# Two equal parts of 16 tiles, q rows of the first part made inside attention, and the last norm on ScalarE

## The chip, the core and the metric

The kernel runs on one core of a Trainium2 chip. The metric is the device time of one execution in microseconds (us), and the median over 13 executions is 1920.35 us. The core has five engines that each work through their own queue in order: TensorE (PE, with its weight loads as PEld), VectorE (DVE), ScalarE (ACT), GpSimd (POOL) and SyncE (SP, which only starts transfers). DMA engines move data between the chip's memory (DRAM) and the on-chip SBUF; TensorE writes to PSUM.

## The reference

One layer of a graph network over 4096 nodes of 512 features, 8 heads of 64. All arithmetic is in float32.

```python
hs = layer_norm(x) * ln1_scale + ln1_bias          # 4096 x 512
ht = layer_norm(h_target) * ln1_scale + ln1_bias
q = (ht @ Wq + bq) / 8;  k = hs @ Wk + bk;  v = hs @ Wv + bv
logits = where(adj != 0, q . k per head, -1e30)     # adj: 4096 x 4096, some 17 edges a row
ctx = softmax(logits) @ v
ht = layer_norm(ht + ctx @ Wo + bo) * ln2_scale + ln2_bias
y = ht + gelu(ht @ W1) @ W2                         # W1 512 x 2048, W2 2048 x 512
out = layer_norm(x + y)                             # no scale, no bias
```

A row of adj has few edges, so the kernel does not form the logits. It makes a list of the neighbours of each target row and gathers their k and v rows.

## The kernel before, in words

**Tiles and parts.** A tile is 128 target rows. The 32 tiles' rows are in two parts: part A, the first 20 tiles of rows, and part B, the last 12. Within a part the rows are sorted by their number of edges, so that the rows of one tile need about the same number of gathers. CAPS_A and CAPS_B are the numbers of gathers for each tile of a part (600 in all). Tiles are taken in groups of two (the first and the last group have one): A tiles with few edges first, then those with more, then B.

**First phase.** Three streams are woven into one program by hand-given costs (`_weave`; each `yield` gives a cost in units, and the stream that is furthest behind goes next; the scheduler of the language then fixes each engine's order with this as its priority).
- `project` handles a list of pairs of tiles. For a pair of x tiles (`source`), the rows are normalised (ACT, line 800), transposed (PE, line 834), scaled and shifted (ACT, line 838), multiplied by Wk and Wv (PE, line 848), copied (ACT, line 850) and written to the table kvd in DRAM. For a pair of h_target tiles (`target`), the same transposes are multiplied by Wq (PE, line 860); DVE applies the scale and bias (line 863), two more operations make the residual rows from the normalised h (lines 868 and 869, on POOL for the first tiles and on DVE for the rest), and both halves go as one row of 1024 values to a table tqd in DRAM (line 871). The order is x pairs, then x and part A's h pairs in turn, then part B's h pairs.
- `edges` reads adj in four quarters for each tile. A quarter (128 x 1024 int32, 512 KB) goes into a tile "a" with two buffers; ACT takes its sign and the row count (line 670); DVE multiplies by an index ramp (line 672) and extracts the positions (line 674 and lines 681 to 698). The first 20 tiles are done in this phase, and more in what `fill` takes.
- `sort` ranks the rows of a part by counting (two pairs of matmuls with scans between, lines 767 to 775) and scatters their lists to DRAM by POOL (line 783).
- `moments` loads a tile of h_target ("hst") and takes its mean and variance on DVE; before, for part B's tiles alone.

When all k and v rows are in kvd and part A's lists are written, the gathers can begin.

**Second phase.** Three streams again: attention, the feed-forward (`feed`), and the lists of part B that are left (`other_lists`).
- `issue` starts the gathers of three edges' rows at a time (POOL, line 896, one gather for each edge position, 512 KB) into the tile kv with six buffers of three slots, four groups ahead of use (AHEAD). For a tile's first group it also gathers the tile's q and residual rows from tqd (`front`).
- For each group of three: DVE multiplies k by q (line 1058) and sums by head (line 1062), ACT takes exp (lines 1066 and 1076; line 1040 and the eight multiplications at line 1043 handle the third slot's v), DVE multiplies v by the weights (line 1023), and PE sums the v rows by transposes that add up in PSUM (cps, line 1031). For tiles of part B, DVE first adds two of the three v rows (line 1027), which saves PE four transposes.
- `finish`, a step at a time, divides by the sum of the weights (lines 957 to 970), multiplies by Wo into the one PSUM bank "t" (line 975), adds the residual on DVE (line 978), normalises (lines 653 and 990), and transposes to h2T (lines 999 and 1003, through "t" again).
- `feed` multiplies h2T by W1 (`hidden`, PE, line 1156), takes Gelu on ACT (line 1159), and multiplies by W2 into po (PE, line 1165). The residual is put into po first by transposes (line 1189).
- `end` adds x (DVE, line 1122), takes mean and variance on DVE (line 653), the power on POOL (line 643), scales on DVE (line 1129), and scatters the rows to the output (POOL, line 1133).

The scalars rstd of the norms are a power of -0.5 on POOL (`power`, line 643).

## Time and profile before

| | us |
|---|---|
| median of 13 runs | 1920.35 |
| lowest, highest | 1909.82, 1925.46 |
| the profiled execution | 1925.34 |
| its span | 1923.6 |
| last matmul ends, in the span | 1904.3 |
| first gather of kv starts, in the span | 405.4 |
| TensorE's first feed-forward matmul, in the span | 505.5 |

The profile is of one execution. Busy time is the time in which an engine executes; an engine that waits for another is idle. A row of a group gives the line in the kernel, the engine, the operation, tile names (out<-in), the shape, the count, the busy time in us and the mean of one in ns, then the idle time ahead of it with what ended it. A matmul of 128 x 512 in float32 shows as two records (passes). The busy time of passes is less than their count times their mean, since they overlap; costs on TensorE are therefore taken as busy time divided by the count. A row of a stretch gives its bounds, its length, and for each engine the busy time and the number of instructions, then the clock granted to TensorE, the mean busy share of the DMA engines and GB/s.

### The profile page before, as it was taken

What the parts mean: (1) busy time and instruction counts of PE and PEld (TensorE: products, weight loads), DVE (VectorE), ACT (ScalarE), POOL (GpSimd) and SP (SyncE); (2) the same over time, 40 slices, a digit from 0 to 9 for tenths busy, and PEclk for the clock granted to TensorE, in tenths of its full rate; (3) what the DMA queues carried; (4) which work ended last, traced back from release to release, by engine and by line L of the source; (5) the groups of instructions that cost most, each with busy time, mean ns of one, the idle gap of its engine ahead of it and who ended that gap; (6) DMA issues with size and microseconds to landing.
All of it is one profiled execution on the core that took longest, in us unless ns stands there. A gap on an engine that the chain in (4) does not pass through costs nothing.

```text
span 1923.6 us, 22615 instructions
## 1 busy us (share of the span) xinstructions
PE 1712.5 (89%) x6974; PEld 1101.5 (57%) x6974; DVE 1503.0 (78%) x2712; ACT 1173.8 (61%) x2937; POOL 951.4 (49%) x847
## 2 busy tenths in 40 slices
PE   7899888787789899988998999888998998999996
PEld 3344344334557566765666666666665765666664
DVE  4778887656989899866677878888999998989601
ACT  5566565444668776656575757676776776766510
POOL 1012232233545445565465656667677776677101
PEclk9999999888989999998999999999999999999998
DMA  8888886698979686757676878788888787778200
GB/s 315 267 270 290 287 267 212 207 351 340 358 285 319 244 305 225 261 180 236 198 272 237 280 245 309 264 293 290 286 300 287 263 302 263 248 260 278 80 1 24
DMA packets 155738, 490.48 MB, mean 255 GB/s; under 512 B 24900, under 2 KB 29592, under 8 KB 155608
## 3 DMA queue, kind: packets, MB, share of 16 engines
q0 software_dynamic: 99040, 355.28, 53.3%
q1 hardware_dynamic: 50864, 114.78, 17.9%
q10 hardware_dynamic: 5704, 18.89, 2.5%
q8 instruction: 57, 0.93, 0.2%
q14 instruction: 73, 0.60, 0.1%
HBM read 441.23 MB, written 47.65 MB: 254 GB/s over the span
## 4 chain that ended last, share of the span: by engine, by line
PE 30%; DVE 25%; DMA 20%; issue 10%; POOL 7%; ACT 5%; another core or an unknown queue 0%; POOLq 0%; SPq 0%; ACTq 0%; DVEq 0%
PE pf L1156 11%; PE po L1165 9%; DMA a<-in_adj_dram 9%; DVE kv L1058 7%; DMA kv<-kvd,rec 7%; DVE lg L1062 6%; PE cps L1031 5%; DVE kv L1023 4%; POOL kv L896 4%; PE t L975 2%; ACT sg L670 1%; POOL rec L783 1%; PE pq L848 1%; DMA xin<-in_L_gnn_h_target_dram 1%; DVE cand L674 1%
## 5 line engine op out<-in xcount | busy, mean ns | idle before, releaser
L896 POOL DMA_INDIRECT kv<-kvd,rec x600 | 702.0, 1170 | 407.8 <-issue 191.7
L1156 PE MATMUL pf<-h2T,w 128*128 128x256 f32 (+1 forms) x2176 | 480.3, 373 | 9.6 <-ACT h2T L1003 5.0
L1165 PE MATMUL po<-w,gt 128*128 128x512 f32 x1024 | 473.6, 601 | 8.1 <-ACT gt L1159 6.7
L1058 DVE TENSOR_TENSOR kv<-kv,tq 128x1536 f32<-128x1536 f32 (+2 forms) x210 | 351.6, 1675 | 145.1 <-DMA kv<-kvd,rec 132.7
L1156 PEld LDWEIGHTS pf<-h2T,w 128*128 128x128 f32 x2176 | 394.9, 194 | 79.5 <-issue 30.5
L1043 ACT ACTIVATE kv<-kv,pa 128x64 f32<-128x64 f32 x1512 | 387.4, 335 | 5.5 <-ACT pa L1040 0.2
L1062 DVE TENSOR_REDUCE lg<-kv 128x24 f32<-128x1536 f32 (+2 forms) x210 | 349.6, 1668 | 1.2
L1031 PEld LDWEIGHTS cps<-ident,kv 128*128 128x128 f32 x2092 | 247.4, 145 | 109.5 <-issue 47.4
L1031 PE MATMUL cps<-ident,kv 128*128 128x128 f32 x2092 | 273.9, 280 | 34.6 <-DVE kv L1023 20.6
L1165 PEld LDWEIGHTS po<-w,gt 128*128 128x128 f32 x1024 | 188.5, 193 | 194.9 <-issue 184.3
L1023 DVE TENSOR_TENSOR kv<-kv,p 128x1024 f32<-128x1024 f32 (+1 forms) x210 | 248.7, 1187 | 14.6 <-ACT p L1066 11.1
L670 ACT ACTIVATE sg<-a 128x1024 uint8<-128x1024 int32 x128 | 135.0, 1055 | 164.2 <-DMA a<-in_adj_dram 141.5
L643 POOL TENSOR_TENSOR n_rs<-n_ve,mhalf 128x2 f32<-128x2 f32 (+2 forms) x61 | 51.6, 846 | 331.2 <-DVE n_ve L636 289.3
L1066 ACT ACTIVATE p<-lg 128x24 f32<-128x24 f32 (+2 forms) x178 | 34.0, 191 | 191.6 <-DVE lg L1062 168.5
L975 PE MATMUL t<-wo,rb 128*128 128x512 f32 x256 | 124.2, 627 | 26.7 <-DVE rb L970 23.5
L848 PE MATMUL pq<-wk,hT 128*128 128x512 f32 x256 | 125.0, 633 | 24.8 <-ACT hT L838 22.8
L1159 ACT ACT_TABLE_LOAD x111 | 142.4, 1283 | 1.9
L848 PE MATMUL pq<-wv,hT 128*128 128x512 f32 x256 | 120.6, 616 | 17.8 <-DVE wd L672 9.6
L860 PE MATMUL pq<-wq,hT 128*128 128x512 f32 x256 | 124.6, 632 | 13.2 <-ACT hT L838 12.6
L1159 ACT ACTIVATE gt<-pf 128x512 f32<-128x512 f32 x128 | 76.4, 597 | 90.5 <-PE pf L1156 76.9
L674 DVE MAX8 cand<-wd 128x8 uint16<-128x103 uint16 (+1 forms) x640 | 128.6, 252 | 1.2
L1066 ACT ACT_TABLE_LOAD x82 | 105.2, 1283 | 26.2 <-DVE lg L1062 15.5
(140 smaller groups left out, 1519.4 us busy)
## 6 DMA issues: line engine op xcount, KB each, us to landing
a<-in_adj_dram SPq DMA_DIRECT2D x128, 512.0 KB
kvd<-row ACTq DMA_DIRECT2D x32, 512.0 KB
tq<-row SPq DMA_DIRECT2D x20, 512.0 KB
kv<-kvd,rec POOLq DMA_INDIRECT x600
xin<-in_L_gnn_h_target_dram SPq DMA_DIRECT2D x16, 512.0 KB
w<-in_L_gnn_W_dram SPq DMA_DIRECT2D x8, 1024.0 KB
xin<-in_x_dram SPq DMA_DIRECT2D x15, 512.0 KB
tq<-row POOLq DMA_DIRECT2D x12, 512.0 KB
```

The lines of the kernel that those rows point to most:

```text
L670: nc.scalar.activation(sg, a, AF.Sign, accum_out=dpart[:, i, h:h + 1])
L848: nc.tensor.matmul(pkv, hT[:, kc, j * P:(j + 1) * P], w[:, kc, :], start=kc == 0, stop=kc == KC - 1)
L896: nc.gpsimd.indirect_dma_start(out=dst, out_offset=None, in_=table[:, :], in_offset=bass.IndirectOffsetOnAxis(ap=idx, axis=0))
L975: nc.tensor.matmul(pa, ct[:, c, :], wo[:, c, :], start=c == 0, stop=c == KC - 1)
L1023: nc.vector.tensor_tensor(v4, v4, p[:, j0:j0 + m, :].unsqueeze(3) .to_broadcast([P, m, H, HD]), ALU.mult)
L1031: nc.tensor.matmul(cps[:, c, :], kv[:, j, D + c * P:D + (c + 1) * P], ident, is_transpose=True, start=j0 + j == 0 and c == 0, stop=j0 + n ...
L1043: nc.scalar.mul(v, v, pa[:, hd:hd + 1])
L1058: nc.vector.tensor_tensor(kv[:, :n, :D], kv[:, :n, :D], tq[:, :D].unsqueeze(1).to_broadcast([P, n, D]), ALU.mult)
L1062: nc.vector.tensor_reduce(lg[:, :n, :], kv[:, :n, :D].rearrange("p j (h d) -> p j h d", h=H), AX.X, ALU.add)
L1156: nc.tensor.matmul(pf[:, k, :], w1[(f0 + k) // KC][:, kc, (f0 + k) % KC * P:((f0 + k) % KC + 1) * P], h2T[:, kc, :w], start=kc == 0, stop= ...
L1159: nc.scalar.activation(gt, pf, AF.Gelu_apprx_tanh)
L1165: nc.tensor.matmul(po[j], gt[:, k, j * P:(j + 1) * P], w2[(f0 + k) // KC][:, (f0 + k) % KC, :], start=False, stop=f0 + k == FC - 1, skip_g ...
```

## The change

What it does, by parts:
1. The parts are 16 and 16 tiles; the caps sum to 603.
2. Only part B's q rows are made in the first phase's `project`, after all x tiles. Its residual rows come from transposing the scaled and shifted hT back on PE, and are copied by ACT; the constant bo + bv Wo is folded into the shift b1r, and its product with Wq is taken off the q bias again.
3. For a tile of part A, `front` gathers the rows of h_target itself in the tile's order, scales them on ACT by the row statistics (now carried in the list record), transposes them, and multiplies by Wq, one step at each `advance` of attention. hT stays beside q in tq. `finish` adds it by four transposes into the bank of the Wo product; ACT copies the sum out, where DVE added. The first two tiles' fronts run ahead of the gathers (EARLY).
4. `moments` runs for all 32 tiles.
5. `end` adds x with an accumulated sum, takes the variance by Square on ACT (which writes over po) and scales by Identity on ACT.
6. kv is a ring of 17 slots, not six buffers of three; adjacency quarters are asked for two ahead; wd is written over sg; gt has two buffers, not three.
7. Costs and order in the weave change; W1 and W2 quarters 2 and 3 are asked for inside the first feed-forward, on ACT's queue.

```diff
-CAPS_A = (40, 24, 23, 22, 21, 20, 20, 19, 18, 18, 17, 17, 16, 16, 15, 15, 14, 13, 12, 11)
-CAPS_B = (38, 23, 21, 20, 19, 18, 17, 16, 16, 15, 14, 12)
+CAPS_A = (39, 24, 23, 22, 20, 19, 19, 18, 17, 17, 16, 15, 15, 14, 13, 11)
+CAPS_B = (38, 24, 23, 22, 20, 19, 18, 18, 17, 17, 16, 15, 15, 14, 13, 12)
+    RING = 17
...
             def late_constants():
...
                 nc.vector.tensor_add(bob, pb, bob)
-                return wq, s1b, bob, bq8
+                yield
+                pt = psi.tile([P, D], F32, name="pq", bufs=3)
+                for kc in range(KC):
+                    nc.tensor.transpose(pt[:, kc * P:(kc + 1) * P], bob[:, kc * P:(kc + 1) * P],
+                                        ident)
...
+                nc.vector.tensor_add(b1r, rbc, b1c)
+                yield
+                pb = psi.tile([P, D], F32, name="pq", bufs=3)
+                for kc in range(KC):
+                    nc.tensor.matmul(pb, rbc[:, kc:kc + 1].to_broadcast([P, P]), wq[:, kc, :],
+                                     start=kc == 0, stop=kc == KC - 1)
+                nc.vector.tensor_sub(bqr, bqr, pb)
...
             def edges(i):
...
-                    a = lp.tile([P, QW], I32, name="a", bufs=2)
-                    nc.sync.dma_start(a, adj[i * P:(i + 1) * P, h * QW:(h + 1) * QW])
+                    n = i * NQ + h
+                    while len(adjs) < min(n + 2, NT * NQ):
+                        adjs.append(quarter(*divmod(len(adjs), NQ)))
+                    a, adjs[n] = adjs[n], None
...
-                    elif h == 3 and moms and NA - i <= len(moms) + 1:
+                    if h % 2 and moms:
                         moments(moms.pop(0))
...
             def sort(part):
...
+                yield 6.0
...
+                yield 4.0
...
-                yield 20.0
+                yield 10.0
...
                 def target(n, j):
...
+                    pr = psi.tile([P, D], F32, name="pq", bufs=3)
+                    for kc in range(KC):
+                        nc.tensor.transpose(pr[:, kc * P:(kc + 1) * P],
+                                            hT[:, kc, j * P:(j + 1) * P], ident)
...
-                    eng, dma = (nc.vector, nc.sync) if ready else (nc.gpsimd, nc.gpsimd)
-                    eng.tensor_mul(tq[:, D:], t[:, j, :], s1b)
-                    eng.tensor_add(tq[:, D:], tq[:, D:], bob)
...
+                    nc.scalar.copy(tq[:, D:], pr)
+                    r0 = (g * G + j - NA) * P
+                    nc.sync.dma_start(tqd[r0:r0 + P, :], tq)
...
             def front(i):
...
+                rec = recs[i]
+                tq = sp.tile([P, 2 * D], F32, name="tq", bufs=3)
+                if TILES[i][0] >= NA * P:
+                    gather(tq, tqd, rec[:, ROW:ROW + 1])
+                    tqs[i] = tq
                     return
...
+                t = tq[:, :D]
+                gather(t, h_target, rec[:, TGT:TGT + 1])
+                yield
+                m = rec[:, RST:RST + 2].bitcast(F32)
+                nc.scalar.activation(t, t, AF.Identity, bias=m[:, 1:2], scale=m[:, 0:1])
+                yield
+                pt = ps.tile([P, KC, P], F32, name="t")
+                for kc in range(KC):
+                    nc.tensor.transpose(pt[:, kc, :], t[:, kc * P:(kc + 1) * P], ident)
+                hT = tq[:, D:].rearrange("p (c t) -> p c t", c=KC)
+                for kc in range(KC):
+                    nc.scalar.activation(hT[:, kc, :], pt[:, kc, :], AF.Identity,
+                                         bias=b1r[:, kc:kc + 1], scale=s1c[:, kc:kc + 1])
+                yield
+                yield
+                pq = ps.tile([P, D], F32, name="t")
+                for kc in range(KC):
+                    nc.tensor.matmul(pq, hT[:, kc, :], wq[:, kc, :], start=kc == 0,
+                                     stop=kc == KC - 1)
+                nc.vector.scalar_tensor_tensor(tq[:, :D], pq, HD ** -0.5, bqr,
+                                               op0=ALU.mult, op1=ALU.add)
                 tqs[i] = tq
...
-                kvs[k] = kp.tile([P, S, 2 * D], F32, name="kv")
+                kvs[k] = ring[:, place[k]:place[k] + n, :]
...
             def finish(i, p, cps, group, hs, mv):
...
+                first = TILES[i][0] < NA * P
+                if first:
+
+                    for c in range(KC):
+                        nc.tensor.matmul(pa[:, c * P:(c + 1) * P],
+                                         tq[:, D + c * P:D + (c + 1) * P], ident,
+                                         is_transpose=True, start=c == 0, stop=False,
+                                         skip_group_check=True)
...
-                nc.vector.tensor_add(h, pa, tq[:, D:])
+                if first:
+                    nc.scalar.copy(h, pa)
+                    yield
+                else:
+                    nc.vector.tensor_add(h, pa, tq[:, D:])
...
                 def advance():
+                    for i in list(fronts):
+                        step(fronts, i)
...
             def end(group, xs, po):
...
-                    nc.vector.tensor_add(xs[j], po[j], xs[j])
-                    stats(sp, xs[j], mv[:, j, :], "n3")
...
+                    nc.vector.scalar_tensor_tensor(xs[j], xs[j], 1.0, po[j], op0=ALU.mult,
+                                                   op1=ALU.add, accum_out=sm[:, j, 0:1])
+                nc.vector.tensor_scalar_mul(sm[:, :nt, 0], sm[:, :nt, 0], -1.0 / D)
                 yield
                 for j in range(nt):
-                    nc.vector.tensor_scalar(xs[j], xs[j], mv[:, j, 0:1], rs[:, j:j + 1],
-                                            op0=ALU.subtract, op1=ALU.mult)
+                    nc.scalar.activation(po[j], xs[j], AF.Square, bias=sm[:, j, 0:1],
+                                         accum_out=sm[:, j, 1:2])
...
+                for j in range(nt):
+                    nc.scalar.activation(xs[j], xs[j], AF.Identity, bias=nm[:, j:j + 1],
+                                         scale=rs[:, j:j + 1])
...
                 last = hidden(0)
+                if g == 0:
+                    load_quarter(wp2, 2, nc.scalar)
...
+                    if len(w1) < 4:
+                        load_quarter(wp2, 3, nc.scalar)
...
+            EARLY = 2
+            PAUSE = 30.0
+            ROWS = 8.0
...
-                    yield 1.9 * cost
+                    yield 1.5 * cost
                 yield from sort(1)
...
-            _weave((att, t0), (chain(feed(g) for g in range(len(GROUPS))), UNIT / 2 + LEAD),
-                   (other_lists(), t0))
+            _weave((att, t0 + PAUSE), (chain(feed(g) for g in range(len(GROUPS))), UNIT / 2 + LEAD),
+                   (other_lists(), t0 - 30.0))
```

## The prediction

> **What bounds the kernel now.** I read the page first, for the busy shares; then the same engines in seven stretches; then one source line in those stretches, for a rate; then what TensorE waited for.
>
> ```profile
> span 1923.6 us, 22615 instructions
> PE 1712.5 (89%) x6974; PEld 1101.5 (57%) x6974; DVE 1503.0 (78%) x2712; ACT 1173.8 (61%) x2937; POOL 951.4 (49%) x847
> ```
>
> TensorE is busy 1712.5 of 1923.6 us, so the span is its work plus 211 us of idling. The stretches say where it idles (columns: stretch, length, busy time of PE, PEld, DVE, ACT, POOL, granted clock, DMA share, GB/s):
>
> ```profile
> 0.00:25.00 25.00, 12.12 (x33) 6.26 (x34) 10.26 (x42) 10.53 (x17) 5.47 (x21) 1.00 0.93 341
> 25.00:125.00 100.00, 93.39 (x237) 42.76 (x236) 71.72 (x300) 61.80 (x115) 4.28 (x6) 0.95 0.83 277
> 125.00:310.00 185.00, 158.69 (x428) 72.89 (x427) 153.31 (x593) 112.36 (x207) 50.40 (x50) 0.96 0.79 266
> 310.00:405.00 95.00, 76.43 (x208) 35.19 (x206) 58.27 (x202) 46.83 (x87) 26.65 (x28) 0.93 0.69 228
> 405.00:505.00 100.00, 74.08 (x242) 40.59 (x242) 71.31 (x97) 41.79 (x125) 49.76 (x42) 0.86 0.93 354
> 505.00:1800.00 1295.00, 1193.30 (x5383) 833.53 (x5384) 1118.04 (x1403) 885.11 (x2364) 803.51 (x687) 0.97 0.78 267
> 1800.00:1924.00 124.00, 104.52 (x449) 70.28 (x447) 20.09 (x81) 15.38 (x28) 11.37 (x13) 0.93 0.05 18
> ```
>
> The first four are the first phase: k and v rows of all x, edge lists, and q rows of part A. By the sums there TensorE idles 405 - 340.6 = 64 us. It ends when the last k/v row has landed (404.6 in the timeline; the first kv gather starts at 405.4). Then come 25.9 us of idling to 505, where the feed-forward begins, 101.7 us to 1800, none in the feed-forward tail, and 19.3 us from the last matmul (1904.3) to the end.
>
> **Part by part. First phase.** The new phase holds only x tiles, lists and row statistics. The stretch 25 to 125 already is such a mix: no q matmul falls in it. There line 848 gives:
>
> ```profile
> 25.00:125.00 100.00, 86.39 (x187) 36.68 (x188) 0.95 0.83 277
> 125.00:310.00 185.00, 100.39 (x214) 40.89 (x212) 0.96 0.79 266
> ```
>
> That is 187 passes of k and v in 100 us; with q tiles in between it is 214 in 185. All x need 513 (16 a tile), and 203 are done at 125. The other 310 at 1.87 a us take 166 us: 291. The new constants (4 transposes, 8 passes) cost 4, the last row's write 8 (7.3 before): the table is complete at **303**, not 404.6. Lists: 56 records on line 670 in that stretch are 28 quarters of 100 us; 30 are done at 125, so the 64 of sixteen tiles end near 245. Before, the last list of part A to the last scatter took 345 - 308 = 37 us: 282. One early q chain is record 2, gather 10.6, scaling 0.8, transposes and copies 2.5, matmuls 3.9, about 20: 302. The lists are thus level with the rows, without slack. Twelve hst loads fall in that stretch, and 32 over 300 us is the same rate; the prefetched adjacency quarters keep two buffers, so I give them nothing (ACT waited 32.9 us for them before 125, but TensorE for ACT only 11).
>
> **TensorE's work**, in busy time per instruction: q costs 124.6/32 = 3.9 us a tile and the transposes of h 0.163 each; moved, not removed. Added: 4 transposes of hT for each B tile (64 x 0.163 = 10.4), 4 into the wo bank for each A tile (64 x 0.155 by line 966 = 9.9), constants 4.5. Removed: with sixteen B tiles the pre-add at line 1027 runs 101 times, not 77, and with 603 slots, not 600, the cps transposes fall from 2092 to 2008: 84 x 0.131 = 11.0. Sum 1726.3. Done at 303: k and v 240.5, x transposes 20.9, constants 8, two early fronts 9: 279. Left: **1447**.
>
> **Idling after 303.** The old 127.6 us, changed as follows.
> ```profile
> PE t L975 <- DVE rb L970: 19.2, 8, 6.4
> PE t L999 <- ACT h2T L1003: 17.1, 6, 6.2
> PE t L999 <- ACT h L990: 13.9, 9, 4.7
> PE cps L1031 <- DVE kv L1027: 9.9, 8, 3.3
> PE t L767 <- DVE a L768: 5.6, 1, 5.6
> ```
> These are TensorE's waits from 560 to 1800 (us in total, times, longest).
> - The sort now yields between its two matmul pairs: the last row goes, -6.
> - Fronts. Fourteen run inside attention. Each puts a gather, an ACT scaling, two uses of the one PSUM bank t and four ACT copies (4 x 0.45) into the queues. Behind the scaling on ACT stand exp, the eight v scalings and Gelu, for which TensorE waits. The trace has no such chain. The bank's present waits are 50 us over some 29 tiles with four uses each, 0.43 a use. Ends: 0, and 14 x 6.4 = 90. By the nearest row, two uses cost 0.9 a tile; half of it lies beside FFN matmuls: +6.
> - The end. DVE loses add, bn_stats, aggregate and scaling (0.68 + 0.69 + 0.17 + 0.57) a tile for one add with accumulation (about 0.76) and small ones: -37 us over 32 tiles. ACT gains Square (0.60, by the Gelu from PSUM, + 0.19 accumulator) and Identity 0.80: +51. Square writes po, so the next group's po transposes (line 1189, idle 0.0 now) wait for two of them and a Gelu, at most 2.2 us x 15 = 33; nearest, a copy with a feed-forward step beside it: +4. The very end is 1.5 longer.
> - The ring of 17 slots holds five groups of three, not six, so a gather waits for the transposes of one group nearer. POOL waits 58 us for cps now and DVE 133 us for gathers, but TensorE only 18 us for DVE's kv. Ends 0 and 18: +3.
> - DVE between 505 and 1800: four more list tiles at 11 us (+44), pre-adds 24 x 0.68 (+16), front +11, h add -11, end -37: +23 on 1118, in a longer stretch. Nothing for it. ACT in all +80 (the 51, copies of h and of hT 18, narrower hT copies 11) on 1174: 65%, hidden by TensorE; without that cover it is the fronts' rival below. DMA loses some 10 MB of 490 at a 0.78 share: nothing. W1 and W2 quarters 2 and 3 go to ACT's queue inside the first feed-forward: 2 MB at 354 GB/s is 6 us, against two steps of it.
>
> Idling: 127.6 - 6 + 6 + 4 + 3 = 135. Sum: 303 + 1447 + 135 + 19.3 + 1.5 = **1906**, against 1923.6: -18. The profiled execution took 1925.3 (span plus 1.7); the median of the 13 runs is 1920.35, 5 lower. So 1920.35 - 18 = **1902**.
>
> Two rules bear on it. After TensorE had idled 5 us at 400 its weight loads on line 860 ran 0.34 us apart by 0.52, and 0.19 by 0.24 from 413:
> ```profile
> 407.33 0.34 PEld L860 LDWEIGHTS pq<-wq,hT 128*128 128x128 f32 x1 [0.52 <-issue]
> 413.32 0.19 PEld L860 LDWEIGHTS pq<-wq,hT 128*128 128x128 f32 x1 [0.24 <-issue]
> ```
> The Trainium skill, "TensorE: Matmul & The Clock Gate" (Part 1: The HAM clock gate), says that an idle window of about 3.4 us halves the clock until some 3.4 us of work have passed. By it every front wait of that length costs about 1.7 us more, an estimate, which speaks against the change; the sum with all fourteen so long would be some 70 us higher. "ScalarE: Activation LUTs" (Table sets) says that cheap functions sit in every set, but does not list Square there. In this trace Identity, Copy and Sign rows bring no loads of their own after the first; a load is 1.283. Ends: none, or two in each of 16 groups, 41 us of ACT time, off TensorE's path; I take none.
>
> **The rivals.**
> 1. The forecast, 1875 to 1917: chance 0.46.
> 2. DVE's relief at the ends takes away TensorE's waits for DVE in attention too (19.2 + 17.6 = 37): 1865. For it: from 1400 to 1800 DVE is 93% busy, beside TensorE. Against: lists and pre-adds give the 37 back. 0.19.
> 3. The first phase doesn't shrink so far: lists and the early fronts come 20 us late, or DMA (0.83 there) holds the rows: 1922, no change. For it: no slack at 302. 0.11.
> 4. Slower: the fronts. In-order ACT waits for the h gather (10.6 us at 417), Gelu and exp are late behind it, and TensorE stops at bank t. At 5.5 us a tile, 77 us instead of 6: 1973. It decides from (18 + 4 + 6)/14 = 2 us a tile. For it: the longest waits at t are 4.7 to 6.4, and a gather is asked for just ahead of the scaling. Against: mean wait 0.43. 0.24.
>
> **Numbers.** 1902. The range 1850 to 1950 takes in the forecast, rival 2 with a little more, rival 3, and the lower half of rival 4; it leaves out some 2 in 10. A measurement of this kernel can tell 0.2% (4 us) from no change: faster 0.64, same 0.11, slower 0.25.
>
> **What would show it.** Right: first kv gather near 303, no line for q in the first 300 us, feed-forward from about 438 (303, the old 74 us of work and 26 of idling there, and 35 more of work: 4 tiles of q, 64 transposes, two fronts), TensorE busy about 1726 and idle about 180 (24 + 135 + 21) in all. Wrong: lists or scatters ending after the last k/v row; TensorE waiting for ACT at bank t by more than 40 us; loads of tables beside Square; DVE waiting for gathers far over 133 us; DVE, not TensorE, without gaps between 500 and 800, where most of part B's lists now lie.

## The result and the profile after

The changed kernel is slower: 1937.23 us median of 11 runs, against 1921.05 for the kernel before on the same chips (48 runs); the ratio is **1.0076**, with a 95% interval of 1.0058 to 1.0094. Ratios here and below are of means, so they differ a little from those of the medians, and one far slower execution on each side (4545 and 2117 us) is left out of this one. The prediction was 1902. The profiled execution of the changed kernel took 1934.43 us, with a span of 1932.7.

The page of the changed kernel, span and busy times:

```profile
span 1932.7 us, 23024 instructions
...
PE 1717.7 (89%) x7030; PEld 1104.6 (57%) x7030; DVE 1444.2 (75%) x2637; ACT 1226.8 (63%) x3097; POOL 903.8 (47%) x804
```

TensorE works 5 us more than before and DVE 59 less. The span is TensorE's work plus 215 us of idling (before: 211). The stretches, with bounds at the first kv gather (336.7) and the first feed-forward matmul (456.7); columns as in the prediction:

```profile
0.00:25.00 25.00, 10.34 (x21) 5.08 (x22) 10.33 (x42) 9.60 (x16) 5.48 (x21) 1.00 0.91 333
25.00:125.00 100.00, 93.39 (x249) 42.68 (x247) 75.70 (x317) 60.71 (x112) 4.42 (x6) 0.98 0.84 283
125.00:336.70 211.70, 170.53 (x434) 76.29 (x435) 136.42 (x559) 115.90 (x217) 32.33 (x31) 0.93 0.79 251
336.70:456.70 120.00, 96.95 (x383) 57.36 (x382) 88.30 (x176) 70.59 (x193) 49.26 (x44) 0.89 0.89 323
456.70:1800.00 1343.30, 1232.81 (x5464) 847.11 (x5463) 1112.89 (x1465) 940.65 (x2508) 800.89 (x690) 0.96 0.76 260
1800.00:1932.70 132.70, 113.68 (x484) 76.08 (x482) 20.55 (x81) 29.39 (x56) 11.39 (x13) 0.94 0.06 18
```

Subtract PE's busy time from the length of each stretch. In the first three TensorE idles 62.4 us (14.66 + 6.61 + 41.17), where it idled 64.8 before. The phase lost 66 us of TensorE's work, 69 us of its length and only 2 us of its idling; the prediction had 24 us of idling there. After the first gather TensorE idles 152.6 us (23.05 + 110.49 + 19.02), where it idled 146.3 before and the prediction had 156. So the gain failed to come in the first phase, and what the rest of the change costs then stands alone.

The ledger of one profiled execution each, by the same subtraction (the experiments follow below). The passes of TensorE are the same 7030 in all rows but before and e13, and their busy time still lies between 1711 and 1718 (in the other runs with as many passes, between 1705 and 1727); differences under some 7 us are left to the timed ratios.

| kernel | first kv gather at | idle before it | idle after it | TensorE busy | span | ratio to before |
|---|---|---|---|---|---|---|
| before | 405.4 | 64.8 | 146.3 | 1712.5 | 1923.6 | 1 |
| the prediction | 303 | 24 | 156 | 1726 | 1906 | |
| changed | 336.7 | 62.4 | 152.6 | 1717.7 | 1932.7 | 1.0076 |
| e3, no early loads of h | 322.3 | 52.0 | 152.6 | 1711.4 | 1915.9 | 0.9991 |
| e15, four adjacency buffers | 330.7 | 57.3 | 152.2 | 1711.8 | 1921.3 | 1.0028 |
| e13, no work in the fronts | 339.3 | 62.9 | 149.2 | 1660.0 | 1872.1 | 0.9731 |
| e8, statistics at use, old end | 321.5 | 49.4 | 141.0 | 1712.6 | 1903.0 | 0.9940 |
| e18, e8 with four buffers | 312.3 | 42.8 | 139.6 | 1712.0 | 1894.4 | 0.9859 |

Where the first phase falls behind is seen from the k/v matmuls alone (now line 878) in the changed kernel: stretch, length, busy time and passes of PE, clock, DMA share, GB/s.

```profile
25.00:125.00 100.00, 81.99 (x181) 0.98 0.84 283
125.00:250.00 125.00, 102.71 (x218) 0.96 0.83 267
250.00:337.00 87.00, 49.73 (x103) 0.88 0.73 227
```

That is 1.81, 1.74 and 1.18 passes a us; the prediction carried 1.87 through to the end. The last k/v pass ended at 323.9, so the 103 passes behind 250 us took 74 us, 1.39 a us. In the last stretch nothing is full: all lines together, DVE is busy 48 of 87 us, ACT 45, PE 63. It is a chain of waits, and the timeline shows the two longest links. ACT (line 695 is an adjacency quarter, 954 the scaling of a front, 868 an x pair's hT), then PE (line 795 is the first matmul of the sort):

```profile
289.27 1.06 ACT L695 ACTIVATE sg<-a 128x1024 uint8<-128x1024 int32 x1 [3.63 <-issue]
290.23 0.19 ACT L695 ACTIVATION_READ_ACCUMULATOR sg<-a 128x1 f32 x1
302.41 0.81 ACT L954 ACTIVATE tq<-tq,rec 128x512 f32<-128x512 f32 x1 [11.99 <-DMA tq<-in_L_gnn_h_target_dram,rec]
303.13 0.56 ACT L880 COPY row<-pq 128x512 f32<-128x512 f32 x1
303.60 0.57 ACT L868 ACTIVATE hT<-t,cols 128x256 f32<-128x256 f32 x1
```
```profile
262.45 0.48 PE L795 MATMUL t<-oh,ones_bf 128*128 128x384 bf16 x1 [9.58 <-DVE a L1362]
290.66 3.60 PE L878 MATMUL pq<-wv,hT 128*128 128x512 f32 x8
304.22 6.36 PE L878 MATMUL pq<-wk,hT 128*128 128x512 f32 x8 [9.96 <-ACT hT L868]
```

TensorE stands 9.6 us at the sort's first matmul, for DVE. Later ACT stands 12 us at the first early front's scaling, for a gather; behind it stand the copies of an x pair that is ready, and TensorE stands 10 us for those. At 1.87 a us the 103 passes would have taken 55 us, not 74: the two stops, 19.5 us, are as long as the difference.

### The profile page after: what moved, and what is told of

It reads as the page before. It is cut to its first block, busy times and chain, and to the rows that moved or that the text cites. A ratio compares the mean times of both kernels' runs of the same rounds, so it can differ in the third digit from the quotient of the medians.

```text
span 1932.7 us, 23024 instructions
## 1 busy us (share of the span) xinstructions
PE 1717.7 (89%) x7030; PEld 1104.6 (57%) x7030; DVE 1444.2 (75%) x2637; ACT 1226.8 (63%) x3097; POOL 903.8 (47%) x804
## 5 line engine op out<-in xcount | busy, mean ns | idle before, releaser
L924 POOL DMA_INDIRECT kv<-kvd,rec x603 | 709.9, 1177 | 485.3 <-PE cps L1111 217.8
L1258 PE MATMUL pf<-h2T,w 128*128 128x256 f32 (+1 forms) x2176 | 474.0, 370 | 3.8 <-DMA w<-in_L_gnn_W_dram 3.8
L1111 PEld LDWEIGHTS cps<-ident,kv 128*128 128x128 f32 x2008 | 237.7, 144 | 102.0 <-issue 56.3
L1111 PE MATMUL cps<-ident,kv 128*128 128x128 f32 x2008 | 264.7, 278 | 31.4 <-DVE kv L1107 18.1
L1103 DVE TENSOR_TENSOR kv<-kv,p 128x1024 f32<-128x1024 f32 (+1 forms) x211 | 249.9, 1190 | 18.7 <-ACT p L1158 16.8
L659 POOL TENSOR_TENSOR n_rs<-n_ve,mhalf 128x2 f32<-128x2 f32 (+2 forms) x51 | 46.5, 913 | 382.9 <-DVE n_ve L652 193.7
L878 PE MATMUL pq<-wk,hT 128*128 128x512 f32 x256 | 123.4, 625 | 19.5 <-ACT hT L868 18.5
L701 DVE MAX8 cand<-sg 128x8 uint16<-128x103 uint16 (+1 forms) x640 | 128.8, 252 | 0.7
L878 PEld LDWEIGHTS pq<-wv,hT 128*128 128x128 f32 x256 | 50.0, 199 | 84.6 <-issue 57.5
```

What stands on the lines that cost most here:

```text
L701: nc.vector.max(cand[:, h * SQ + s, :], wd[:, w0:w1])
L878: nc.tensor.matmul(pkv, hT[:, kc, j * P:(j + 1) * P], w[:, kc, :], start=kc == 0, stop=kc == KC - 1)
L924: nc.gpsimd.indirect_dma_start(out=dst, out_offset=None, in_=table[:, :], in_offset=bass.IndirectOffsetOnAxis(ap=idx, axis=0))
L1103: nc.vector.tensor_tensor(v4, v4, p[:, j0:j0 + m, :].unsqueeze(3) .to_broadcast([P, m, H, HD]), ALU.mult)
L1111: nc.tensor.matmul(cps[:, c, :], kv[:, j, D + c * P:D + (c + 1) * P], ident, is_transpose=True, start=j0 + j == 0 and c == 0, stop=j0 + n ...
L1258: nc.tensor.matmul(pf[:, k, :], w1[(f0 + k) // KC][:, kc, (f0 + k) % KC * P:((f0 + k) % KC + 1) * P], h2T[:, kc, :w], start=kc == 0, stop= ...
```

## The experiments

Each ratio is against the kernel before on the same chip, with its 95% interval; 0.1% is 1.9 us.

### The first phase

**e3_no_moments** leaves out the h loads and statistics of 31 of the 32 tiles (all tiles take the first one's mean and variance); **e17_loads_only** keeps the loads and leaves out those statistics.

```diff
 def moments(i):
+    if i:                                   # e17: after the load
+        nc.vector.tensor_copy(mvh[:, i, :], mvh[:, 0, :])
+        return
     t = ip.tile([P, D], F32, name="hst", bufs=1)
     nc.sync.dma_start(t, h_target[i * P:(i + 1) * P, :])
```

> The changed kernel, leaving out the loads of h_target and the row statistics of 31 of the 32 tiles (the first tile's stand in for all): 8 MB and 27 us of VectorE less in the first 270 us. Theory A: what TensorE waits for is not those loads; the first kv gather moves by less than 8 us and the time by less than 8. Theory B: 8 of some 80 MB less brings the end of the first phase forward by 20 to 30 us, and the time falls by 15 to 25 us.

> The changed kernel with the 32 early loads of h_target kept and their statistics left out for all but the first tile (the others copy its mean and variance, so the rows are scaled by wrong factors). Theory that the 8 MB more in DMA hold the first phase: first gather 333 to 337 as in the changed kernel, ratio 1.005 to 1.0076. Theory that VectorE, in order behind a load that has not come (29.5 us in 10 waits), is late for the lists: first gather near 322 as without both, ratio near 0.999.

Measured: e3 0.9991 (0.9972 to 1.0010), first gather 322.3; e17 1.0051 (1.0026 to 1.0075), first gather 331.8. DVE's waits for hst in order, in total, times and longest, in the changed kernel and in e17:

```profile
DVE n_st L669 <- DMA hst<-in_L_gnn_h_target_dram: 29.5, 10, 5.4
```
```profile
DVE n_st L669 <- DMA hst<-in_L_gnn_h_target_dram: 4.8, 1, 4.8
```

e17 takes 25 us of DVE's waits away and gains 0.25%, with an interval that overlaps the changed kernel's; e3 takes the bytes away too and gains 0.85%, 16 us. The 8 MB of early loads cost most of it, DVE's place behind them less. Whether it is their bytes or their place in SyncE's queue that costs is not parted: SyncE stands 63 us at line 761 in the changed kernel, waiting until the one buffer hst is free (40.7 us in e17), and e3 takes that away too.

**e12_no_prefetch** asks for an adjacency quarter in its own step, as before the change.

```diff
-                    while len(adjs) < min(n + 2, NT * NQ):
-                        adjs.append(quarter(*divmod(len(adjs), NQ)))
-                    a, adjs[n] = adjs[n], None
+                    a = quarter(i, h)
```

> The changed kernel with each adjacency quarter asked for in its own step, as before, not two ahead. The record gave the prefetch nothing: ratio 1.004 to 1.011, first kv gather within 5 us of 337. Theory A (ScalarE behind Sign): without it ScalarE waits longer for quarters, the first kv gather comes 5 to 15 us later. Theory B (load): the loads of x come earlier in their place and the first phase gets no longer or shorter.

Measured 1.0084 (1.0053 to 1.0116): asking early with the same two buffers is worth nothing that can be told in time. ACT does wait longer for quarters without it (117.5 us in the first 345, against 91.2 in the first 340), and the first gather came at 342.6, 6 us later than in the changed kernel, as theory A had it.

**e2_four_quarters** gives the quarters four buffers and asks four ahead. The memory for it was taken from the ring (15 slots); **e6_ring15** has the short ring alone.

```diff
-    RING = 17
+    RING = 15                               # e2 and e6
-                a = lp.tile([P, QW], I32, name="a", bufs=2)
+                a = lp.tile([P, QW], I32, name="a", bufs=4)     # e2
-                while len(adjs) < min(n + 2, NT * NQ):
+                while len(adjs) < min(n + 4, NT * NQ):          # e2
```

> The changed kernel with four buffers for adjacency quarters and four asked for ahead (two and two before), and a kv ring of 15 slots in place of 17 to make room; 15 holds five groups of three just as 17 does. Theory A: ScalarE's waits for adjacency in the first 320 us (85 us) fall below 30, TensorE's waits for copies and hT (34 us in that phase) fall by 15 or more, and the first kv gather comes near 315, not 337; the time falls by 10 to 20 us unless the ring costs. Theory B: more quarters in flight only slow the other transfers; first kv gather within 6 us of 337, time within 5 us of 1937.

> The changed kernel with a kv ring of 15 slots in place of 17; both hold five groups of three, but 17 has room for a short group beside them. It prices the ring inside the run with four adjacency quarters, where the second phase idled some 17 us more than in the changed kernel. If the ring did that, this is 6 to 15 us slower than the changed kernel (ratio 1.011 to 1.015); if not, within 3 us of it (1.006 to 1.009).

Measured: e2 1.0104 (1.0073 to 1.0135), first gather 325.0; e6 1.0199 (1.0159 to 1.0239). With 15 slots there are 28 places, near a wrap, where a group takes slots of one of the four groups ahead of it that is still to be used: some groups compute with other rows, and their gathers wait. So neither time is a price of the ring, and e2 is no clean test of the buffers, though its first gather is.

**e15_four_clean** puts the two more buffers into memory that only the first phase uses, and keeps the ring.

```diff
-                a = lp.tile([P, QW], I32, name="a", bufs=2)
+                n = i * NQ + h
+                if n < 64 and n % 4 > 1:
+                    a = ip.tile([P, QW], I32, name="a2", bufs=2)
+                else:
+                    a = lp.tile([P, QW], I32, name="a", bufs=2)
...
-                    while len(adjs) < min(n + 2, NT * NQ):
+                    while len(adjs) < min(n + (2 if n > 59 else 4), NT * NQ):
```

> The changed kernel with four adjacency buffers in the first phase, asked for four ahead, and nothing else changed (the ring stays at 17). Theory that ScalarE, in order behind an adjacency quarter (85 us of waits), holds back the copies for which TensorE waits: those waits fall under 50 us, first gather near 325 instead of 337, ratio 0.9995 to 1.003. Theory that DMA's rate itself holds the first phase: the same bytes take as long, first gather 333 to 337, ratio 1.005 to 1.008.

Measured 1.0028 (1.0004 to 1.0052), first gather 330.7. ACT's waits for adjacency up to 340 us, in the changed kernel and in e15, and the next cause in e15:

```profile
ACT sg L695 <- DMA a<-in_adj_dram: 91.2, 44, 6.7
```
```profile
ACT xin L833 <- DVE n_nm L664: 35.2, 12, 11.3
ACT sg L699 <- DVE cand L705: 24.5, 16, 4.3
ACT sg L699 <- DMA a<-in_adj_dram: 20.9, 5, 14.6
```

70 of 91 us of that wait are gone and 0.48% is gained. But ACT now waits 60 us for DVE at these two lines, 11.5 in the changed kernel, and TensorE's waits for ACT's hT and row are no shorter. The changed kernel from 125 to 340 us, then e15 (lines 795 and 799 are the sort's first matmul):

```profile
PE pq L878 <- ACT hT L868: 15.0, 6, 10.0
PE pq L878 <- ACT row L880: 12.5, 6, 3.0
PE t L795 <- DVE a L1362: 9.6, 1, 9.6
```
```profile
PE pq L882 <- ACT hT L872: 23.3, 7, 10.6
PE pq L882 <- ACT row L884: 6.6, 2, 6.3
PE t L799 <- DVE a L800: 0.2, 1, 0.2
```

So it is not shown that ACT's order behind adjacency held the copies for TensorE (27.5 us of these waits, then 29.9). The wait that is gone is the one at the sort: the last scatter of part A's lists ran at 282.5, not 291.7. The two buffers bring the lists forward by 9 us and the first gather by 6; the time stands with the first theory, the gather half way, and that theory's path is not what the trace shows.

**e1_front_later** puts two more steps between a front's gather and its scaling; **e14_no_early** starts no front ahead of the gathers.

```diff
                 gather(t, h_target, rec[:, TGT:TGT + 1])
                 yield
+                yield                       # e1
+                yield
```
```diff
-                for i in range(EARLY):
+                for i in range(0):          # e14
                     fronts[i] = front(i)
```

> The changed kernel with two more steps between the gather of the h rows and their scaling in each of the 16 fronts. Theory A (ScalarE works in order; it stands behind a transfer, the gather in front of the scaling and the adjacency quarter in front of Sign, and what TensorE needs stands behind that): ScalarE's 45 us of waiting for the h gather falls under 10, TensorE's 10 us of idling at 294 to 304 goes, and the time falls by 10 to 25 us to some 1912 to 1927. Theory B (the first phase takes as long as its transfers and VectorE's work, whatever stands where): the k/v table is complete at 337 as before, and the time stays within 4 us of 1937.

> The changed kernel with no front ahead of the gathers: the two first tiles' fronts start with their own rows. Theory that the early scaling, in order on ScalarE ahead of the last x pair's copies, holds the table: the wait of 10 us of TensorE at the end of the x tiles goes, the first gather comes near 327, not 337; the first front then stands in attention's own start, which takes most of it back: 1.003 to 1.007. Rival, that the wait is only a symptom and the rows are late anyway: first gather still 335 or later and the feed-forward starts 10 us later than 457, ratio 1.012.

Measured: e1 1.0072 (1.0047 to 1.0096), e14 1.0060 (1.0035 to 1.0085). Neither edit moved the stop, so neither run tells what it costs. In e1 ACT still stood 13.0 us at the scaling. In e14 the first front still asked for its rows at 297.2, 37 us ahead of the first kv gather (334.7), and ACT and TensorE stood as in the changed kernel:

```profile
301.71 0.81 ACT L954 ACTIVATE tq<-tq,rec 128x512 f32<-128x512 f32 x1 [12.26 <-DMA tq<-in_L_gnn_h_target_dram,rec]
303.52 6.41 PE L878 MATMUL pq<-wk,hT 128*128 128x512 f32 x8 [10.45 <-ACT row L880]
```

The stop is older than the fronts. While the records of part A are scattered, SyncE, which asks for adjacency, x and h, asks for nothing: next in its queue stands a load that reads the records back. SyncE's transfers in the kernel before, then in the changed kernel:

```profile
331.61 0.33 SPq L667 DMA_DIRECT2D a<-in_adj_dram  x1
349.14 0.38 SPq L1100 DMA_DIRECT2D degs<-rec  x1
```
```profile
284.53 0.45 SPq L732 DMA_DIRECT2D rest_d<-gid  x1
293.86 0.80 SPq L938 DMA_DIRECT2D rec<-rec  x2
```

SyncE's waits name the scatter (rec<-R,ranki) in e15, then in e12:

```profile
SPq L1196 <- DMA rec<-R,ranki: 14.7, 1, 14.7
```
```profile
SPq L1187 <- DMA rec<-R,ranki: 16.8, 1, 16.8
```

In the changed kernel the DMA engines' share is 0.06 from 290 to 295 us. ACT meanwhile stands at whatever is next: at an adjacency quarter for 15.6 us before, 15.2 in e12 and 14.6 in e15, at the front's scaling for 12.0 in the changed kernel. TensorE then stands 9.6 us before, 9.2 in e12, 10.6 in e15 and 10.0 in the changed kernel. No run takes this stop away, so its price is not measured.

### The fronts

**e9_no_front_work** and **e13_plain_rows** replace a front's work by a second gather of h rows. Left out in both: the scaling, the transposes, the q product and the copies of part A, so q is a raw row. In e13 exp takes a factor of 1/8.

```diff
-                t = tq[:, :D]
-                gather(t, h_target, rec[:, TGT:TGT + 1])
-                yield
...
+                for c in range(2):
+                    gather(tq[:, c * D:(c + 1) * D], h_target, rec[:, TGT:TGT + 1])
                 tqs[i] = tq
...
-                                nc.scalar.activation(p[:, :n, :], lg[:, :n, :], AF.Exp)
+                                nc.scalar.activation(p[:, :n, :], lg[:, :n, :], AF.Exp,
+                                                     scale=HD ** -0.5)     # e13
```

> The changed kernel, leaving out the scaling, the transposes and the q matmuls of the fronts of part A: each gathers its rows of h_target into both halves of tq and that is all (part A is computed from unscaled rows). TensorE's work in them is 70 us (60.0 for the matmuls, 10.0 for the transposes in the changed kernel's profile). The record's step: the fronts cost their work and some 6 us of waiting, so the time falls by 70 to 85 us, to a ratio of 0.963 to 0.971. The record's fourth rival: their waits at the bank t and behind ScalarE cost 40 to 77 us more, so it falls by 110 to 150 us, a ratio of 0.93 to 0.95.

> The changed kernel without the work of part A's fronts: two gathers of rows of h_target fill both halves of tq, with no scaling, no transposes, no q matmuls and no copies (exp takes a factor of 1/8 instead, so that the sums stay small). Left out: the norm, the scale and shift, and the q product of part A. Theory that the fronts cost their TensorE work alone: about 57 us less than the changed kernel, 1880 on the scale of 1920 before, ratio 0.979, TensorE idling 195 to 205 us before the last matmul, as with the fronts (196). Rival 4 of the prediction (TensorE's waits for the fronts are what ate the gain): the listed waits of 39 us go too, 1840, ratio 0.96 or less, idling 160 or less.

e9 took 7828.67 us, because the large sums of exp sent it through the general path after the fast one; its ratio says nothing. Up to its last feed-forward matmul (1856.9, 57 us earlier) TensorE idled 201 us, as against 196. e13 measured 0.9731 (0.9683 to 0.9778), 3.45% or 66 us less than the changed kernel. Its page:

```profile
span 1872.1 us, 22589 instructions
...
PE 1660.0 (89%) x6838; PEld 1078.4 (58%) x6838; DVE 1432.5 (77%) x2621; ACT 1203.0 (64%) x3025; POOL 921.0 (49%) x820
```

58 us of TensorE's work are gone and 3 of its idling (212 against 215). Up to the last matmul it idles 202 us, against 196 with the fronts; the rest is an end of 9.9 us, not 18.7, for which no run shows a reason. The changed kernel does list waits for the fronts, and without the fronts others stand in their place. TensorE's waits from 450 us to the last feed-forward matmul, in the changed kernel, then in e9:

```profile
PE cps L1111 <- DVE kv L1107: 18.1, 7, 5.3
PE t L1077 <- ACT h2T L1081: 15.9, 5, 5.1
PE t L1043 <- ACT tq L961: 15.5, 4, 6.8
PE t L1077 <- ACT h L1068: 14.7, 9, 5.5
```
```profile
PE cps L1093 <- DVE kv L1085: 26.2, 8, 8.6
PE t L1059 <- ACT h L1050: 21.4, 13, 7.2
PE t L1059 <- ACT h2T L1063: 21.0, 9, 6.2
PE cps L1093 <- DVE kv L1089: 16.8, 6, 4.4
```

The 15.5 us for line 961 (the front's hT) go, and the waits for DVE's kv are 43.0 - 22.8 = 20 us longer (with 4.7 us of the changed kernel at line 1103), those for ACT's h and h2T 42.4 - 30.6 = 12. The prediction's sign of rival 4, over 40 us of TensorE's waits for ACT at bank t, does stand in the changed kernel (56 us), but also in e9 (46), which has no fronts. Rival 4 falls.

### The end, the ring, the order

**e4_end_dve** is the changed kernel with the old end on DVE; **e5_before_end_act** is the kernel before with the new end alone.

```diff
-                    nc.scalar.activation(po[j], xs[j], AF.Square, bias=sm[:, j, 0:1],
-                                         accum_out=sm[:, j, 1:2])
...
+                    nc.vector.tensor_add(xs[j], po[j], xs[j])
+                    stats(sp, xs[j], mv[:, j, :], "n3")
```

> The changed kernel with the last norm back on VectorE as before (add, bn_stats, aggregate, scaling). The record's step: the new end costs TensorE some 4 us at po and the very end 1.5, so this would be 0 to 6 us faster. Rival: the 37 us that VectorE is spared are worth TensorE's waits for VectorE in the second half, and this is 10 to 25 us slower than 1937.

> The kernel before with one part of the change alone: the last norm on ScalarE (Square into po, Identity). If the new end has a price of its own, as putting the old one back into the changed kernel says (ratio 1.0038, not 1.0076, some 7 us), this is 4 to 10 us slower than before, with TensorE's waits for ScalarE (h, h2T) longer in the second half. If its price hangs on the fronts that also load ScalarE, this is within 3 us of before.

Measured: e4 1.0038 (1.0017 to 1.0059), so the new end costs 0.38% or 7 us in the changed kernel; e5 1.0062 (1.0039 to 1.0084), 12 us in the kernel before. TensorE's wait for Gelu at line 1165 of before, which is 1175 in e5:

```profile
PE po L1165 <- ACT gt L1159: 6.7, 3, 3.2
```
```profile
PE po L1175 <- ACT gt L1169: 13.6, 7, 4.3
```

DVE fell from 371.9 to 351.7 busy us in 1400 to 1800, and TensorE idled 27.3 us there, not 21.4. Over the run TensorE's waits for DVE at rb and kv fell from 54 to 37 us, and the time rose. So DVE's relief bought nothing, and the new end on ACT cost. At the transposes into po, where the prediction had the price, TensorE waited only 0.5 us for Square.

**e10_before_ring17** is the kernel before with the ring of 17; **e11_no_pause** is the changed kernel with the second phase's streams started as before.

```diff
+            ring = kp.tile([P, RING, 2 * D], F32, name="kv")        # e10
-                kvs[k] = kp.tile([P, S, 2 * D], F32, name="kv")
+                kvs[k] = ring[:, place[k]:place[k] + n, :]
```
```diff
-            _weave((att, t0 + PAUSE), (chain(feed(g) for g in range(len(GROUPS))), UNIT / 2 + LEAD),
-                   (other_lists(), t0 - 30.0))
+            _weave((att, t0), (chain(feed(g) for g in range(len(GROUPS))), UNIT / 2 + LEAD),
+                   (other_lists(), t0))
```

> The kernel before with the ring of 17 slots alone. The ring of 15 was no clean measure: in it a group can take slots of a group that is still to be used, so rows of some groups are other ones and gathers wait for more than the ring's size. The record's step: 3 us, between 0 and 18 (ratio 1.000 to 1.009). If POOL's longer waits for the transposes (79 us before, 218 after) count, 8 to 18 us slower.

> The changed kernel with the second phase's weave started as before (attention not 30 units later, lists not 30 units earlier). If the order in the weave is worth something, it shows in TensorE's idling from 337 to 1000 (74 us in the changed kernel) and the ratio leaves 1.003 to 1.012 on either side; if not, it stays in there. No theory of mine says which; the record gave the order no price.

Measured: e10 0.9996 (0.9977 to 1.0016), the ring costs nothing that can be told; e11 1.0131 (1.0097 to 1.0164), so the new starts of the second phase's streams are worth 0.55%, 11 us, for which the prediction had no term.

### A version that beats both

**e7_stats_at_use** takes the early loads away: part B's statistics come from the pair that `target` loads anyway, part A's from the rows that the front has gathered. **e8_stats_end_dve** is e7 with the old end; **e16_best_scale_dve** is e8 with the fronts' scaling on DVE; **e18_best_four** is e8 with e15's buffers.

```diff
-                m = rec[:, RST:RST + 2].bitcast(F32)
-                nc.scalar.activation(t, t, AF.Identity, bias=m[:, 1:2], scale=m[:, 0:1])
+                nc.vector.bn_stats(f[:, 0:6], t)
+                nc.vector.bn_aggr(f[:, 6:8], f[:, 0:6])
...
+                nc.scalar.activation(t, t, AF.Identity, bias=f[:, 10:11], scale=f[:, 9:10])
```

> The changed kernel without the 32 early loads of h_target: the row statistics of a part B tile are taken from the tile that its q matmuls load anyway, and those of a part A tile from the rows that its front gathers (bn_stats, POOL power and two more steps in each front). Theory B (load sets the end of the first phase): as in the run that left the loads out, first kv gather near 322, ratio 0.999 to 1.003. Theory A (what stands behind a transfer): the longer chain in the fronts makes more waits at the PSUM bank t, 16 x 1 to 2 us, and ratio stays at 1.005 or above.

> The same, and the last norm back on VectorE. If the two prices add (16 us for the early loads less a little for the longer fronts, 7 us for the new end), the ratio is 0.993 to 0.999, faster than before; if both are the same wait seen twice, it is no better than either alone, 0.999 to 1.003.

> The version with statistics at use and the old end, with the fronts' scaling on VectorE instead of ScalarE. If ScalarE's order behind the gather (exp, v scalings and Gelu standing behind the scaling) costs TensorE time: idling from 435 to 1000 falls from 56 to 45 or less and the ratio is 0.988. If the order on ScalarE costs nothing: 0.994, or up to 0.998 as VectorE has the work and the wait instead.

> The version with statistics at use and the old end, with the same four adjacency buffers in the first phase. If ScalarE's waits for adjacency hold the first phase there too: first gather near 311 instead of 321, ratio 0.988 to 0.990. If DMA's rate or nothing of it does: first gather 318 to 323, ratio 0.993 to 0.995.

Measured: e7 1.0019 (0.9997 to 1.0041); e8 0.9940 (0.9920 to 0.9960); e16 0.9942 (0.9915 to 0.9969); e18 **0.9859** (0.9828 to 0.9890), with medians of 1896.21 us against 1920.00. e7 moves the first gather to 317.7, though a part is lost again behind it: from there to 1000 us TensorE idles 88 us, in the changed kernel 74. That the fronts' longer chain is the reason is likely, not shown. e16 shows that ACT's order behind the fronts' gathers costs nothing that can be told. e18 by stretches:

```profile
25.00:125.00 100.00, 95.89 (x262) 44.40 (x261) 86.98 (x381) 73.23 (x138) 4.63 (x6) 1.00 0.89 306
125.00:312.30 187.30, 165.35 (x429) 75.77 (x428) 117.10 (x490) 105.42 (x196) 31.68 (x37) 0.95 0.70 231
```

TensorE idles 22 us from 125 to the first gather, not 41: with the loads gone and four quarters on their way the phase comes within 9 us of the prediction's 303. The wait at the sort's first matmul is 0.3 us (7.8 in e8), the last scatter of part A runs at 263.1 (277.3 in e8), and the longest stop behind it is 6.6 us.

## Why the prediction was wrong

**The step that failed** is the first phase's: "The other 310 at 1.87 a us take 166 us: 291", with which the table was to be complete at 303. It came at 336.7, 34 us late, and 24 us of idling were 62.4. The rate was read in a stretch in which TensorE was 93% busy, and carried on as if nothing but TensorE's work lay ahead. In the changed kernel 191 passes were done at 125 us, not 203; the next 218 came at 1.74 a us; the last 103 took 74 us, with the two stops of the sort in them (9.6 us at its first matmul, 10.0 behind its scatter). The last pass ended at 323.9, 29 us later than the prediction's 295. The write of its row was asked for 4.5 us after that, since the copy stood on ACT behind an h pair's scaling, which waited 3.75 us for its load. The kernel before had the same two stops, 6.4 and 9.6 us, but later than 300 us, outside the stretch from which the rate was read; the prediction gave the sort a time for the lists and none for TensorE.

The runs price two things that lengthen the phase: the early loads of h (16 us, e3), of which the prediction said only that they came at the same rate as in that stretch, and the two adjacency buffers (9 us by e15, 16 in the best version by e18 against e8). The prediction gave adjacency nothing, since TensorE's own wait for ACT was small. That wait did not shrink with four buffers; what went is TensorE's stop at the sort's first matmul, which the prediction had not looked at. How the 34 us divide between the loads, adjacency and the scatter's stop, and what sets the 42.8 us of idling that are left in e18, stays open.

That the lists would be level with the rows was nearly right for the lists: the last scatter of part A ran at 291.7 (predicted 282). The last row's write was asked for at 328.4 and took its 8 us, so the rows were late, not the lists. This is the case of rival 3, the phase that doesn't shrink so far, with 34 us instead of its 20 and a chance of 0.11. Of its two causes, DMA is shown only as far as the loads go, and the lists came ahead of the rows. That the measured time still lies between 1850 and 1950 is luck: the slower half of that range was there for the fronts.

**TensorE's work.** Predicted 1726, measured 1717.7: right, within the spread of one profile.

**Idling after the first gather.** Predicted 156 with the end, measured 152.6: right as a sum, by errors that cancel. Of its terms: the fronts' +6 does not show (up to the last matmul TensorE idles no less without their work, e13); the end's 5.5 was too small (7 by e4, 12 by e5), and neither part of it is where it was put: TensorE doesn't wait at the transposes into po (0.5 us in e5, nothing in the changed kernel), its wait for Gelu grows instead (by 7 us in e5), and the very end is not longer (18.7 us, 19.1 before); the ring's +3 is 0 (e10); the sort's -6 was 4, since 1.7 us are left of the 5.6 in the second phase; and the new starts of the streams, without which the kernel is 11 us slower (e11), had no term. TensorE's wait for DVE's rb at line 975 of before, 23.5 us, fell to 4.0 at its line 1048 now, but DVE's relief did not become time (rival 2 falls by e5).

**Nothing for prefetched quarters** was right for the time (e12). **No table loads beside Square** was right: loads stand at the lines of exp and Gelu alone, 211 in all against 221 before, and the first one of line 829.

**The sum.** 1932.7 - 1906 = 27: the first phase's idling +38.4, TensorE's work -8, idling after the gather -3. With the first phase's idling as in the changed kernel the prediction's own terms give 1944 in the span, slower than before. All of the forecast's gain hung on one extrapolated rate.

**The clock.** The row at 304.22 above shows what a stop costs beyond itself: after 9.96 us of idling eight passes took 6.36 us, against 3.60 for eight passes ahead of it, so 2.8 us more; the granted clock was 0.50 from 300 to 305 us and 0.54 from 305 to 310, after 1.00 from 285 to 290. The Trainium skill, "TensorE: Matmul & The Clock Gate" (Part 1: The HAM clock gate), by which the prediction estimated 1.7, agrees in kind, and the row is longer. Over the whole execution the mean granted clock was 0.956 before and 0.955 after, so this made no difference between the kernels.

## What to carry to other kernels

When work moves out of a phase, ask first whether that phase's idling belongs to the work or to the queues that stay: here 66 us of TensorE's work left and the idling stayed. A rate from a stretch at 93% may be extrapolated only over work like that of the stretch: here the sort lay ahead, and its two stops of 19.5 us were not in the rate. Look in each queue for a transfer that has to wait, and at what stands behind it: SyncE's read of the records kept adjacency, x and h waiting. A list of waits for one new step is not its price: TensorE stopped for other engines as long when the step was gone.

## What had not been expected

- Two adjacency buffers more, 1 MB, in memory that stood free in the first phase, are worth 0.5% to 0.8%, about as much as the new end costs (0.4% and 0.6%).
- Asking for a transfer earlier without another buffer was worth nothing (1.0084 against 1.0076).
- The kernel before already had the 10 us stop behind the scatter; it stayed when the q rows left the phase.
- 8 MB of loads cost 12 to 16 us in a phase in which the DMA engines were busy at a mean share of only 0.79 to 0.84.
